# Layer 0 of a four-layer image network: where the 2x2 parity order of the pixels is made, how the row maxima are cut, and in which order a step's parts stand on each engine

## The chip, the core and the metric

The kernel runs on one core of a Trainium2 chip. The metric is the device time of one execution in microseconds (us); the time of a version is the median of three runs. One further execution is taken with the hardware profiler, and all durations below come from that one. The engines are called PE (TensorE, the matrix engine; PEld is its weight load, which overlaps the matmul before it), DVE (VectorE), ACT (ScalarE), POOL (GpSimd) and SP (SyncE, which only issues transfers).

## The reference, cut to what matters

The input `x` is 8 images of 128 channels and 56x56 pixels, float32. Four layers follow one another, each as `x = x + layer(group_norm(x))`, with 32 groups. The change touches layer 0 alone, an attention in which every window looks at four windows chosen for it:

```python
xw   = windows(gn(x))                      # 49 windows of 8x8 pixels per image, 128 channels
q, k, v = split(xw @ W_qkv + b_qkv)        # 128 channels each
logit = (q.mean(pixels) * SCALE) @ k.mean(pixels).T      # 49 x 49
r_idx = top_k(logit, 4)                    # four windows for each window
k_sel, v_sel = k[r_idx], v[r_idx]          # 4 * 64 = 256 keys
attn = softmax(q_h * SCALE @ k_sel.T)      # 8 heads of 16 channels, 64 queries x 256 keys
o    = attn @ v_sel
lepe = depthwise_3x3(image(v)) + lepe_b    # 3x3 convolution of each channel by itself
out  = (o + lepe) @ W_o + b_o
```

Layer 1 is a tanh recurrence over the 3136 pixels of an image, layer 2 a masked 3x3 convolution with a 1x1 one, layer 3 a block of two 3x3 convolutions.

## The kernel before

**Units.** `X` holds all 8 images on chip, 128 channels on the partitions. An image is 7 blocks of 448 pixels, a block one row of 7 windows; there are 56 blocks and 392 windows, worked on in 196 pairs. `xw` holds the normalised pixels of one image by windows, `kT` (called `ks` when it is read) its keys, `q` the queries of one block, once for each head of a pair of heads with the other's channels masked. The values go to memory as rows of pixels (`vpix`) and are fetched window by window into the buffer `ring`; they also go to memory as an image (`vimg`) from which the depthwise convolution is read (`v3`).

**Parity order.** Within a window the 64 pixels do not stand in reading order but sorted by the parity of row (`a`) and of column (`c`): four groups of 16. The depthwise convolution and the transposes of 32 channels need it. `normalise` (L287 to L292) makes this order as it writes `xw`, with one instruction for each of the four groups; the end of `project` (L483 to L487) takes it apart again as it adds the result to `X`, again with four.

**A step.** The loop over `p` from -3 to 201 works on several pairs at once. In step `p`:

- `scores(p+2)` (L570): PE multiplies the queries of two windows with their 256 gathered keys, for four groups of 32 channels, into four banks of PSUM called `s0` to `s3`. `maxima(p+2, g)` (L577): DVE takes the maximum over the keys, one instruction of 512 elements for each bank. `halve(p+2)` (L583, L584): POOL splits the negated maxima into two bfloat16 halves. `flip(p+2)` (L589): PE transposes them into bank `t2`; `flipped(p+2)` (L593): ACT copies them to `nm`.
- `shifted(p+1)` (L602, L612): PE writes the negated maxima of the pair before, and on top of them the transposed scores, into four banks `t0` to `t3`. `exponentials(p+1, g)` (L622): ACT, one for each bank.
- `values(p)` (L636): PE multiplies the exponentials with the fetched values, into `po`, which lies in bank `s0`. `turned` and `divide` (L648, L657, L660): DVE transposes the sums and divides by the denominators, into `ot`.
- `join(p-2)` (L465): POOL adds the depthwise result to `ot`. `back(p-2)` (L471): DVE transposes the sum into `outs`, by channels again.
- `gather(2p+6)` (L534): POOL copies the keys of the chosen windows, eight copies. `fetch(p+2)` (L549): SP, ACT and POOL issue the transfers of the chosen values.

**Jobs.** Beside these parts a step does up to one job in each of three places, `one`, `two` and `light`: the work that is done once for each block or image. A job has a part on PE and an end on other engines. Per block these are keys (L305, end on ACT L311), image (L316, end on ACT L322, then transfers), pixels (L339, end L358 on), queries (L410, end in two ACT instructions L415), depthwise (L443, end on DVE: memset L449 and transpose L451; the loads of the next block's `v3`, L429, are issued by POOL in the step after), and project (L481, end in four DVE instructions L487; the transfer `xkeep` L488 is issued by POOL in the step after). Per image come a group's mean and variance and the choice of windows. Where depthwise is placed (56 steps) it takes the place `two` and the step is called longer.

A list of jobs with the step in which each is ready and the step in which it is due is sorted by due step, and each step takes the first that is ready for each place. Instructions without a job of their own on PE (normalise, its sums L297, statistics L226 and L496) are put in steps by a weight, so that DVE's load is even.

**Order.** PE, ACT, DVE and POOL run their instructions in the order in which the program issues them (a manual schedule). Within a step that order is written out by hand in two strings, `SHORT` and, for steps with depthwise, `LONGER`. A table `SLOTS` says which bank of PSUM each part uses:

```python
SLOTS = dict(values=(ps_s, "s0"), flip=(ps_t, "t2"), one=(ps_t, "t0"), two=(ps_t, "t1"),
             light=(ps_s, "s2"), tails=(ps_s, "s1"))
SHORT = """fetch0 scores shifted gather join max0 max1 values exp0 max2 exp1 max3 halve ahead one light two flip exp2
    root back turned divide end1 exp3 flipped lit hooks tails end2 fetch1"""
```

`ahead` issues what was left over from the step before (loads of `v3`, `xkeep`), `end1` and `end2` are the ends of the jobs, `lit` that of the light one, `hooks` the instructions without a job.

Of the kernel before, what the change touches and what calls it, by code (L numbers as in the profile page):

```python
# [20 lines left out]
P = 128  # L21
# [29 lines left out]
def conv_stack_kernel(ctx: ExitStack, tc: tile.TileContext, a: dict, out: bass.AP):  # L51
# [81 lines left out]
    with ExitStack() as l0:  # L133
# [69 lines left out]
        banks = itertools.cycle([(ps, f"{k}{g}") for k, ps in (("s", ps_s), ("t", ps_t)) for g in range(4)])  # L203
# [69 lines left out]
        def preparation(b):  # L273
# [9 lines left out]
            def normalise(i, scalar=False):  # L283

                dst = xw[:, i * NW : (i + 1) * NW, :].rearrange("p j (a c u v) -> p a c u j v", a=2, c=2, u=4)
                src = X[:, b, i * BLK : (i + 1) * BLK].rearrange("p (u a j v c) -> p a c u j v", u=4, a=2, v=4, c=2)
                for k in itertools.product(range(2), range(2)):  # L287
                    to, x = dst[:, k[0], k[1]], src[:, k[0], k[1]]
                    if scalar:
                        nc.scalar.activation(to, x, AF.Identity, bias=st["off"], scale=st["r"])  # L290
                    else:
                        nc.vector.tensor_scalar(to, x, st["gm"], st["r"], ALU.subtract, ALU.mult)  # L292
# [20 lines left out]
            def image_mm(i):  # L313
                st["pv", i] = psum([P, 4 * WS // 2, NW, WS // 2], f"pvt_{b}_{i}")
                x = xw[:, i * NW : (i + 1) * NW, :].rearrange("p j (s v) -> p s j v", v=WS // 2)
                nc.tensor.matmul(st["pv", i], wvi, x, start=True, stop=True)  # L316
# [88 lines left out]
        def queries(b, i):  # L405
            st = {}

            def mm():
                st["pq"] = psum([P, BLK], f"pq_{b}_{i}")
                nc.tensor.matmul(st["pq"], wqkv[:, :P], xwf[:, i * BLK : (i + 1) * BLK], start=True, stop=True)  # L410

            def end():
                q = qs[b, i] = strip.tile([P, NW, 2, WPX], F32, name=f"q_{b}_{i}", tag="q", bufs=2)
                for h in range(2):
                    nc.scalar.activation(  # L415
                        q[:, :, h], st["pq"].rearrange("p (j x) -> p j x", x=WPX), AF.Identity,
                        bias=qbias[:, h : h + 1], scale=qscale[:, h : h + 1],
                    )
# [54 lines left out]
        def project(b, i):  # L473
# [3 lines left out]
            def mm():  # L477
                st["py"] = psum([P, 2, 2, 4, HW // 2], f"py_{b}_{i}")
                at = (b * NBLK + i) % 2 * NW
                x = outs[:, at : at + NW].rearrange("p j (s v) -> p s j v", v=WS // 2)  # L480
                nc.tensor.matmul(st["py"].rearrange("p a c u (j v) -> p (a c u) j v", v=WS // 2), wo, x, start=True, stop=True)  # L481

            def end():  # L483
                x = X[:, b, cols].rearrange("p (u a x c) -> p a c u x", u=4, a=2, c=2)
                for k in itertools.product(range(2), range(2)):
                    to, y = x[:, k[0], k[1]], st["py"][:, k[0], k[1]]
                    nc.vector.scalar_tensor_tensor(to, y, bo2, to, ALU.add, ALU.add)  # L487
# [71 lines left out]
        def scores(p):  # L559
# [3 lines left out]
                s=[ps_s.tile([P, 2, TOPK * WPX], F32, name=f"s_{p}_{g}", tag=f"s{g}") for g in range(4)],  # L563
                nmax=win.tile([P, 2, 4], F32, name=f"nmax_{p}", tag="nmax"),
            )
            for o in range(2):
                w = wins[2 * p + o]
                for g in range(4):
                    h = slice(g * CL, (g + 1) * CL)
                    nc.tensor.matmul(  # L570
                        s_["s"][g][:, o, :], w["qm"][h].rearrange("p h x -> p (h x)"), w["kw"][h],
# [3 lines left out]
        def maxima(p, g):  # L575
            s_ = pairs[p]
            nc.vector.tensor_reduce(s_["nmax"][:, :, g], s_["s"][g], AX.X, ALU.max, negate=True)  # L577
# [152 lines left out]
        for f in (image[0], image[1], *pixels[1:]):  # L730
# [3 lines left out]
                     light=(ps_s, "s2"), tails=(ps_s, "s1"))  # L734
# [9 lines left out]
        hook(-1, lambda: neighbours(0, 0))  # L744
# [10 lines left out]
        for b in range(B):  # L755
            for i in range(NBLK):
                q, last = pair_of(b, i * NW), pair_of(b, i * NW + NW - 1)
                if b or i > 1:
                    job(max(pair_of(b, i * NW - NW - 1) - 1, -1), q - 3, lambda b=b, i=i: queries(b, i))
# [1219 lines left out]
```

## Time and profile before

| | |
|---|---|
| median of three runs | 3303.14 us (3300.36 to 3306.16) |
| profiled execution | 3306.33 us |
| its span (first to last instruction) | 3304.5 us |
| mean granted clock of TensorE | 0.988 of full speed |
| layer 0 | the first 1190 us or so of the span |
| PE busy, span | 3143.1 us, 95% |
| DVE busy, span | 2327.2 us, 70% |
| POOL busy, span | 1482.2 us, 45% |
| ACT busy, span | 1280.1 us, 39% |
| in the first 1190 us: PE, DVE, POOL, ACT busy | 1081.33, 975.38, 903.43, 661.67 us |

"Busy" is the time in which an engine runs an instruction; issuing transfers, register work and waiting are not counted. Matmuls are pipelined, so that PE can be busy without being at its peak. In a row such as `L577 DVE TENSOR_REDUCE nmax<-s`, L577 is the line of the kernel, DVE the engine, and then come the operation, what it writes and what it reads. A stretch `200:1100` is given in us from the start of the span.

### The profile page before, as it was taken

Reading aid. Unit: us, or ns where it says so; the run is one execution under the profiler, and the core shown is the slowest. Engines: PE = TensorE matmul, PEld = TensorE weight load, DVE = VectorE, ACT = ScalarE, POOL = GpSimd, SP = SyncE. Lnnn points to the kernel's source line nnn. Section 1 sums busy time; section 2 is a strip of 40 time slices with the busy share of each in tenths; the row PEclk is TensorE's granted clock in tenths of the full one; section 3 lists DMA queues with packets and bytes.
Section 4 is the critical chain, followed back from the end, with each engine's and each line's share of the span. In section 5 each row is a group of like instructions: output and inputs, shape, how many; then the busy total and the mean of one; then the engine's idle time right before and its main releaser. Section 6 shows DMA issues by size and latency. Waiting matters only on the chain.

```text
span 3304.5 us, 105617 instructions
## 1 busy us (share of the span) xinstructions
PE 3143.1 (95%) x41230; PEld 2707.2 (82%) x41230; DVE 2327.2 (70%) x6160; ACT 1280.1 (39%) x2432; POOL 1482.2 (45%) x4034
## 2 busy tenths in 40 slices
PE   7999999999998889999999999999999999999998
PEld 5767767776776679999999999999999953499988
DVE  5888888888887866655555555555523257799999
ACT  4555555555565522222111111111112144455654
POOL 4788878877787743333222222222200065322221
PEclk8999999999999999999999999999999999999999
DMA  5566666656566511110000000000022156300001
GB/s 149 129 148 144 145 140 138 149 135 140 128 142 147 114 56 52 49 49 22 1 1 1 1 1 1 1 1 1 21 62 59 52 151 159 87 25 35 30 30 41
DMA packets 196045, 242.76 MB, mean 73 GB/s; under 512 B 46368, under 2 KB 140864, under 8 KB 195536
## 3 DMA queue, kind: packets, MB, share of 16 engines
q0 software_dynamic: 47104, 126.87, 15.9%
q1 hardware_dynamic: 131632, 102.06, 11.5%
q10 hardware_dynamic: 16800, 6.97, 1.0%
q8 instruction: 328, 5.37, 0.7%
q14 instruction: 181, 1.48, 0.2%
HBM read 137.21 MB, written 67.56 MB: 62 GB/s over the span
## 4 chain that ended last, share of the span: by engine, by line
PE 67%; DVE 18%; POOL 5%; issue 5%; ACT 2%; DMA 2%; ACTq 1%; POOLq 1%; DVEq 0%; SPq 0%
PE ps L1112 27%; PE q L1077 9%; PE po L1142 5%; PE po L636 5%; PE t L612 3%; PE pc L1353 3%; PE s L570 3%; PE pi L1047 3%; DVE nmax L577 2%; POOL ks L534 1%; PE pc3b L1599 1%; PE t L602 1%; PE pc L1361 1%; PE pvp L339 1%; DVE u_pc3b L1718 1%
## 5 line engine op out<-in xcount | busy, mean ns | idle before, releaser
L1112 PE MATMUL ps<-hs,w_gates 128*128 128x136 f32 x7680 | 928.8, 279 | 0.0
L1112 PEld LDWEIGHTS ps<-hs,w_gates 128*128 128x128 f32 x7680 | 911.6, 190 | 4.5
L1126 ACT ACTIVATE hs<-v 128x272 f32<-128x272 f32 x538 | 212.3, 404 | 1167.6 <-DVE v L1124 1167.4
L622 ACT ACTIVATE e<-t 128x512 f32<-128x512 f32 x784 | 431.3, 596 | 397.6 <-PE t L612 302.5
L1124 DVE TENSOR_TENSOR v<-ps,g 128x272 f32<-128x272 f32 x538 | 216.4, 411 | 495.5 <-PE ps L1112 409.2
L577 DVE TENSOR_REDUCE nmax<-s 128x2 f32<-128x512 f32 x784 | 485.4, 682 | 78.4 <-PE s L570 76.9
L1065 POOL TENSOR_TENSOR d<-inp 128x136 f32<-128x136 f32 x186 | 87.8, 472 | 789.4 <-DVE inp L1053 789.4
L534 POOL COPY ks<-kT 128x64 f32 x1568 | 293.5, 236 | 142.2 <-PE t L612 93.5
L636 PE MATMUL po<-e,ring 128*32 128x64 f32 x12544 | 250.1, 231 | 23.6 <-DVE nmax L577 13.4
L636 PEld LDWEIGHTS po<-e,ring 128*32 128x32 f32 x12544 | 220.8, 149 | 51.6 <-DVE nmax L577 19.3
L570 PE MATMUL s<-ks,q 32*128 32x256 f32 x3136 | 240.4, 409 | 10.0 <-ACT vp L362 6.1
L612 PE MATMUL t<-q,ks 32*128 32x128 f32 x6272 | 242.0, 275 | 6.4 <-issue 6.4
L612 PEld LDWEIGHTS t<-q,ks 32*128 32x128 f32 x6272 | 223.7, 190 | 11.9 <-issue 8.6
L1599 PE MATMUL pc3b<-vb,u_w2c_t 128*128 128x196 f32 x1152 | 202.2, 338 | 19.9 <-DVE vb L1580 19.9
L1599 PEld LDWEIGHTS pc3b<-vb,u_w2c_t 128*128 128x128 f32 x1152 | 198.7, 195 | 22.2 <-DVE vb L1580 22.0
L1599 PE MATMUL pc3a<-va,u_w1c_t 128*128 128x196 f32 x1152 | 199.9, 334 | 8.1 <-DVE d_pc3a L1616 4.1
L1599 PEld LDWEIGHTS pc3a<-va,u_w1c_t 128*128 128x128 f32 x1152 | 195.1, 193 | 12.0 <-issue 9.7
L1142 PE MATMUL po<-hs,xw 128*128 128x272 f32 x744 | 204.1, 397 | 0.4 <-ACT hs L1126 0.2
L570 PEld LDWEIGHTS s<-ks,q 32*128 32x128 f32 x3136 | 149.9, 188 | 45.5 <-issue 7.6
L1077 PE MATMUL q<-d,mixed 128*128 128x136 f32 x1116 | 160.2, 279 | 0.5 <-DVE g L1091 0.3
L429 POOL DMA_DIRECT2D v<-vimg x224 | 147.6, 665 | 13.7 <-issue 13.3
L1142 PEld LDWEIGHTS po<-hs,xw 128*128 128x128 f32 x744 | 132.0, 190 | 22.4 <-ACT hs L1126 1.0
(307 smaller groups left out, 5394.3 us busy)
## 6 DMA issues: line engine op xcount, KB each, us to landing
v<-vimg POOLq DMA_DIRECT2D x216, 232.0 KB
ring<-vpix SPq DMA_DIRECT2D x1176, 32.0 KB
kept<-g SPq DMA_DIRECT2D x56, 272.0 KB, 2.1
g<-kept SPq DMA_DIRECT2D x56, 272.0 KB, 2.7
xkeep<-X POOLq DMA_DIRECT2D x56, 224.0 KB
vimg<-vrow POOLq DMA_DIRECT2D x108, 116.0 KB
out_dram<-u_pc3b SPq DMA_DIRECT2D x31, 392.0 KB, 2.4
vpix<-vp POOLq DMA_DIRECT2D x42, 256.0 KB
```

What stands on the lines that cost most here:

```text
L534: nc.gpsimd.tensor_copy(kw[:, t : t + 1, :], ks[b][:, bass.ds(at, 1), :])
L570: nc.tensor.matmul(s_["s"][g][:, o, :], w["qm"][h].rearrange("p h x -> p (h x)"), w["kw"][h], start=True, stop=True,)
L577: nc.vector.tensor_reduce(s_["nmax"][:, :, g], s_["s"][g], AX.X, ALU.max, negate=True)
L612: nc.tensor.matmul(s_["t"][g][:, o, c], w["kw"][h, c * P : (c + 1) * P], w["qm"][h].rearrange("p h x -> p (h x)"), start=False, stop=(o == ...
L622: nc.scalar.activation(s_["e"][g], s_["t"][g], AF.Exp)
L636: mm = nc.tensor.matmul(po[g * CL : (g + 1) * CL, h, :, o], flat[:, at : at + 8 * CL - 7 : 8], s_["e"][g][:, o, c, h * WPX : (h + 1) * WPX ...
L1077: nc.tensor.matmul(q[n // 3][:, n % 3], w, x, start=True, stop=True)
L1112: nc.tensor.matmul(ps[f][:, i], whh[:, k, m * P : (m + 1) * P], prev[k // 2][:, (s - 1) % 2, k % 2].rearrange("p c b -> p (c b)"), start=( ...
L1124: nc.vector.tensor_tensor(v[:, i : i + n], ps[f][:, i : i + n], x, ALU.add)
L1126: nc.scalar.activation(to, x, AF.Tanh)
L1142: nc.tensor.matmul(po, wout[:, k, :], hs[k // 2][:, :, k % 2], start=(k == 0), stop=(k == KH - 1))
L1599: nc.tensor.matmul(bank[:, half].rearrange("p (y x) -> p y x", x=H4), u[:, dy, k, :], v[:, k, i * RB + dy : i * RB + dy + RB, :], start=(d ...
```

## The change

It touches layer 0 only.

- `xw`, and with it `kT`'s source, keeps the pixels of a window in reading order: `normalise` is one instruction of 448 elements instead of four of 112.
- The matmuls of image, queries and project are cut in four of 112 columns. Image and queries read `xw`, and project reads `outs`, with strides, one parity group at a time. Image writes the group to its place in the bank; project writes its bank with a step of two, so that the bank holds reading order, and its end is one instruction of 448 instead of four.
- The two ends of the queries bring `q` to parity order: the first half stays on ACT, the second half is a DVE instruction.
- The four score banks become two tiles of two banks each, `s0` and `s1`, and the maxima two instructions of 1,024 elements. `po` lies in `s0` as before, whose tile is now two banks; `light` goes from `s2` to `s1`.
- `join` and `back` work on pair `p-1` instead of `p-2`, and `join` stands ahead of `gather`.
- The strings of a step's order are written anew: `flip` ahead of the second job, `one` ahead of it in `SHORT` and `two` in `LONGER`; `turned`, `divide` ahead of `back`.
- Ready and due steps of queries, depthwise and project are moved, and `neighbours(0, 0)` by one step.

```diff
             return pe, end or (lambda: None), scalar
-        banks = itertools.cycle([(ps, f"{k}{g}") for k, ps in (("s", ps_s), ("t", ps_t)) for g in range(4)])
+        banks = itertools.cycle([(ps_s, "s0"), (ps_s, "s1")] + [(ps_t, f"t{g}") for g in range(4)])
         begun = []
         def psum(shape, name, dtype=F32):
...
             def normalise(i, scalar=False):
-                dst = xw[:, i * NW : (i + 1) * NW, :].rearrange("p j (a c u v) -> p a c u j v", a=2, c=2, u=4)
-                src = X[:, b, i * BLK : (i + 1) * BLK].rearrange("p (u a j v c) -> p a c u j v", u=4, a=2, v=4, c=2)
-                for k in itertools.product(range(2), range(2)):
-                    to, x = dst[:, k[0], k[1]], src[:, k[0], k[1]]
-                    if scalar:
-                        nc.scalar.activation(to, x, AF.Identity, bias=st["off"], scale=st["r"])
-                    else:
-                        nc.vector.tensor_scalar(to, x, st["gm"], st["r"], ALU.subtract, ALU.mult)
+                dst = xw[:, i * NW : (i + 1) * NW, :].rearrange("p j (u v) -> p j u v", v=WS)
+                src = X[:, b, i * BLK : (i + 1) * BLK].rearrange("p (u j v) -> p j u v", u=WS, v=WS)
+                if scalar:
+                    nc.scalar.activation(dst, src, AF.Identity, bias=st["off"], scale=st["r"])
+                else:
+                    nc.vector.tensor_scalar(dst, src, st["gm"], st["r"], ALU.subtract, ALU.mult)
             def sums(i):
...
             def image_mm(i):
                 st["pv", i] = psum([P, 4 * WS // 2, NW, WS // 2], f"pvt_{b}_{i}")
-                x = xw[:, i * NW : (i + 1) * NW, :].rearrange("p j (s v) -> p s j v", v=WS // 2)
-                nc.tensor.matmul(st["pv", i], wvi, x, start=True, stop=True)
+                x = xw[:, i * NW : (i + 1) * NW, :].rearrange("p j (u a v c) -> p a c u j v", u=4, a=2, c=2)
+                for k in itertools.product(range(2), range(2)):
+                    to = st["pv", i][:, 8 * k[0] + 4 * k[1] : 8 * k[0] + 4 * k[1] + 4]
+                    nc.tensor.matmul(to, wvi, x[:, k[0], k[1]], start=True, stop=True)
             def image_end(i):
...
             st = {}
             def mm():
-                st["pq"] = psum([P, BLK], f"pq_{b}_{i}")
-                nc.tensor.matmul(st["pq"], wqkv[:, :P], xwf[:, i * BLK : (i + 1) * BLK], start=True, stop=True)
+                st["pq"] = psum([P, 2, 2, 4 * NW, 4], f"pq_{b}_{i}")
+                x = xwf[:, i * BLK : (i + 1) * BLK].rearrange("p (u a v c) -> p a c u v", a=2, v=4, c=2)
+                for k in itertools.product(range(2), range(2)):
+                    nc.tensor.matmul(
+                        st["pq"][:, k[0], k[1]], wqkv[:, :P], x[:, k[0], k[1]], start=True, stop=True
+                    )
             def end():
                 q = qs[b, i] = strip.tile([P, NW, 2, WPX], F32, name=f"q_{b}_{i}", tag="q", bufs=2)
-                for h in range(2):
-                    nc.scalar.activation(
-                        q[:, :, h], st["pq"].rearrange("p (j x) -> p j x", x=WPX), AF.Identity,
-                        bias=qbias[:, h : h + 1], scale=qscale[:, h : h + 1],
-                    )
+                x = st["pq"].rearrange("p a c (j u) v -> p (a c) j (u v)", u=4)
+                to = [q[:, :, h].rearrange("p j (k x) -> p k j x", k=4) for h in range(2)]
+                nc.scalar.activation(to[0], x, AF.Identity, bias=qbias[:, 0:1], scale=qscale[:, 0:1])
+                nc.vector.tensor_scalar(to[1], x, qscale[:, 1:2], qbias[:, 1:2], ALU.mult, ALU.add)
             return fill(mm, end)
...
             st, cols = {}, slice(i * BLK, (i + 1) * BLK)
             def mm():
-                st["py"] = psum([P, 2, 2, 4, HW // 2], f"py_{b}_{i}")
+                st["py"] = psum([P, 4, 2, HW // 2, 2], f"py_{b}_{i}")
                 at = (b * NBLK + i) % 2 * NW
-                x = outs[:, at : at + NW].rearrange("p j (s v) -> p s j v", v=WS // 2)
-                nc.tensor.matmul(st["py"].rearrange("p a c u (j v) -> p (a c u) j v", v=WS // 2), wo, x, start=True, stop=True)
+                x = outs[:, at : at + NW].rearrange("p j (a c u v) -> p a c u j v", a=2, c=2, v=4)
+                for k in itertools.product(range(2), range(2)):
+                    nc.tensor.matmul(
+                        st["py"][:, :, k[0], :, k[1]].rearrange("p u (j v) -> p u j v", v=4),
+                        wo, x[:, k[0], k[1]], start=True, stop=True,
+                    )
             def end():
-                x = X[:, b, cols].rearrange("p (u a x c) -> p a c u x", u=4, a=2, c=2)
-                for k in itertools.product(range(2), range(2)):
-                    to, y = x[:, k[0], k[1]], st["py"][:, k[0], k[1]]
-                    nc.vector.scalar_tensor_tensor(to, y, bo2, to, ALU.add, ALU.add)
+                nc.vector.scalar_tensor_tensor(
+                    X[:, b, cols], st["py"].rearrange("p u a x c -> p (u a x c)"), bo2, X[:, b, cols], ALU.add, ALU.add
+                )
                 later.append(lambda: nc.gpsimd.dma_start(xkeep[b][:, cols], X[:, b, cols]))
             return fill(mm, end)
...
             s_ = pairs[p] = dict(
-                s=[ps_s.tile([P, 2, TOPK * WPX], F32, name=f"s_{p}_{g}", tag=f"s{g}") for g in range(4)],
+                s=[ps_s.tile([P, 2, 2, TOPK * WPX], F32, name=f"s_{p}_{k}", tag=f"s{k}") for k in range(2)],
                 nmax=win.tile([P, 2, 4], F32, name=f"nmax_{p}", tag="nmax"),
             )
             for o in range(2):
...
                 for g in range(4):
                     h = slice(g * CL, (g + 1) * CL)
                     nc.tensor.matmul(
-                        s_["s"][g][:, o, :], w["qm"][h].rearrange("p h x -> p (h x)"), w["kw"][h],
+                        s_["s"][g // 2][:, g % 2, o], w["qm"][h].rearrange("p h x -> p (h x)"), w["kw"][h],
                         start=True, stop=True,
                     )
-        def maxima(p, g):
+        def maxima(p, k):
             s_ = pairs[p]
-            nc.vector.tensor_reduce(s_["nmax"][:, :, g], s_["s"][g], AX.X, ALU.max, negate=True)
+            to = s_["nmax"][:, :, 2 * k : 2 * k + 2].rearrange("p o g -> p g o")
+            nc.vector.tensor_reduce(to, s_["s"][k], AX.X, ALU.max, negate=True)
         def halve(p):
...
             run(f)
         nc.scalar.activation(root, eps, AF.Exp)
         SLOTS = dict(values=(ps_s, "s0"), flip=(ps_t, "t2"), one=(ps_t, "t0"), two=(ps_t, "t1"),
-                     light=(ps_s, "s2"), tails=(ps_s, "s1"))
+                     light=(ps_s, "s1"), tails=(ps_s, "s1"))
         def second():
...
         hook(-1, lambda: tails.append(second))
         for i in range(3, NBLK):
             job(-1, min(pair_of(0, (i - 2) * NW) + 1, 2 * i), lambda i=i: image[i], True)
-        hook(-1, lambda: neighbours(0, 0))
+        hook(-2, lambda: neighbours(0, 0))
         def offset():
...
             for i in range(NBLK):
                 q, last = pair_of(b, i * NW), pair_of(b, i * NW + NW - 1)
                 if b or i > 1:
-                    job(max(pair_of(b, i * NW - NW - 1) - 1, -1), q - 3, lambda b=b, i=i: queries(b, i))
-                job(q + 1, q + 1, lambda b=b, i=i: depthwise(b, i), True, LONG)
-                job(last + 3, last + 5, lambda b=b, i=i: project(b, i), name=("project", b, i))
+                    job(max(q - 5, -1), q - 5 + (i < 4 and not b), lambda b=b, i=i: queries(b, i))
+                job(q, q, lambda b=b, i=i: depthwise(b, i), True, LONG)
+                job(last + 2, last + 4, lambda b=b, i=i: project(b, i), name=("project", b, i))
         for b in range(1, B):
             at = [FIRST + 1] * NBLK if b == 1 else [pair_of(b - 2, 0) + 2 * i - 1 for i in range(NBLK)]
...
         ih, hh = vecs[:, at : at + KH], vecs[:, at + KH : at + 2 * KH]
         hook(END // 2 + 10, lambda: nc.vector.tensor_add(bg, ih, hh))
-        SHORT = """fetch0 scores shifted gather join max0 max1 values exp0 max2 exp1 max3 halve ahead one light two flip exp2
-            root back turned divide end1 exp3 flipped lit hooks tails end2 fetch1"""
-        LONGER = """fetch0 scores shifted gather join max0 max1 values exp0 max2 exp1 max3 halve ahead two exp2 root back
-            turned divide end2 flip light one exp3 flipped lit hooks tails end1 fetch1"""
+        SHORT = """fetch0 scores shifted join gather max0 values exp0 max1 exp1 halve ahead one exp2 light flip exp3
+            flipped two root turned divide back lit end1 hooks tails end2 fetch1"""
+        LONGER = """fetch0 scores shifted join gather max0 values exp0 max1 exp1 halve ahead two exp2 light flip exp3
+            flipped one root turned divide end2 back lit hooks tails end1 fetch1"""
         def ahead(p):
             for f in later:
...
             if 0 <= p + 2 < END:
                 acts.update(scores=lambda: scores(p + 2), halve=lambda: halve(p + 2), flip=lambda: flip(p + 2),
                             flipped=lambda: flipped(p + 2))
-                for g in range(4):
-                    acts[f"max{g}"] = lambda g=g: maxima(p + 2, g)
+                for k in range(2):
+                    acts[f"max{k}"] = lambda k=k: maxima(p + 2, k)
             if 0 <= p + 1 < END:
                 acts["shifted"] = lambda: shifted(p + 1)
                 for g in range(4):
...
             if 0 <= p < END:
                 acts.update(values=lambda: values(p), root=lambda: root_table(p), turned=lambda: turned(p),
                             divide=lambda: divide(p))
-            if 0 <= p - 2 < END:
-                acts.update(join=lambda: join(p - 2), back=lambda: back(p - 2))
+            if 0 <= p - 1 < END:
+                acts.update(join=lambda: join(p - 1), back=lambda: back(p - 1))
             if p >= 0 and p + 2 < END:
                 acts.update(fetch0=lambda: fetch(p + 2, False), fetch1=lambda: fetch(p + 2, True))
             if p + 3 < END:
```

## The prediction

> **What bounds the kernel now.** I read the page first, for the whole.
>
> ```profile
> span 3304.5 us, 105617 instructions
> PE 3143.1 (95%) x41230; PEld 2707.2 (82%) x41230; DVE 2327.2 (70%) x6160; ACT 1280.1 (39%) x2432; POOL 1482.2 (45%) x4034
> ```
>
> TensorE is the bound, but only layer 0 changes, so the second view is busy time by stretch (columns: stretch, length, then busy time and instructions of PE, PEld, DVE, ACT, POOL; clock, DMA share, GB/s), and the third the instructions of the maxima.
>
> ```profile
> 200.00:1100.00 900.00, 836.34 (x20539) 636.44 (x20541) 761.68 (x1925) 515.55 (x997) 718.33 (x2287) 0.99 0.61 141
> ```
>
> ```profile
> L577 DVE TENSOR_REDUCE nmax<-s x784: 629/681/694, 37.7 to 1171.1; 128x2 f32<-128x512 f32 x196
> ```
>
> Four maxima make a step, so 196 steps take (1171.1-37.7)/195 = 5.81 us each. PE is busy 93% of them, DVE 85%, POOL 80%. To see what a step must take and what it loses, I read TensorE's timeline at a clean step:
>
> ```profile
> 629.39 1.15 PE L570 MATMUL s<-ks,q 32*128 32x256 f32 x16
> 631.68 1.27 PE L636 MATMUL po<-e,ring 128*32 128x64 f32 x64
> 632.87 1.02 PE L305 MATMUL pk<-xw,wqkv 128*128 128x448 f32 x2
> 633.73 0.92 PE L316 MATMUL pvt<-xw,wvi 128*128 128x448 f32 x2
> 634.48 0.28 PE L589 MATMUL flip<-ident,halves 128*128 128x128 bf16 x2
> 634.69 0.50 PE L570 MATMUL s<-ks,q 32*128 32x256 f32 x4
> ```
>
> By differences of starts: scores to values 2.29, values 1.19, a first job 0.86, a second 0.75, flip 0.21; together 5.30. A step with no disturbance needs 3.69 plus its jobs. Next, the timeline of all engines where queries are the second job, and what follows:
>
> ```profile
> 645.58 0.28 PE L589 MATMUL flip<-ident,halves 128*128 128x128 bf16 x2
> 645.78 1.15 PE L570 MATMUL s<-ks,q 32*128 32x256 f32 x16
> 645.94 0.37 ACT L593 COPY nm<-flip 128x256 bf16<-128x256 bf16 x1 [0.75 <-PE flip L589]
> 646.21 1.34 ACT L415 ACTIVATE q<-pq,qbias,qscale 128x448 f32<-128x448 f32 x2
> 646.86 1.07 DVE L292 TENSOR_SCALAR xw<-X,gm,r 128x112 f32<-128x112 f32 x4
> 647.61 0.39 PE L602 MATMUL t<-nm,ones 2*128 2x512 bf16 x3 [0.23 <-ACT q L415]
> 647.85 2.48 DVE L577 TENSOR_REDUCE nmax<-s 128x2 f32<-128x512 f32 x4
> 648.82 1.25 PE L636 MATMUL po<-e,ring 128*32 128x64 f32 x64
> 651.03 0.31 DVE L471 STREAM_TRANSPOSE outs<-ot 128x128 f32<-128x128 f32 x1 [0.70 <-POOL ot L465]
> 651.75 0.28 PE L589 MATMUL flip<-ident,halves 128*128 128x128 bf16 x2
> ```
>
> Scores to values now take 648.82-645.78 = 3.04: 0.75 lost, because ACT freed the queries' bank (t1) only at 647.55. Over all steps between 200 and 1,100 us, starts of scores to starts of values average 2.70, so 0.41 is lost there per step, 2.9 us per seven steps (seven steps are two blocks of 448 pixels). DVE also sits idle 0.70 for the sum (join), in all:
>
> ```profile
> DVE outs L471 <- POOL ot L465: 59.9, 73, 2.6
> ```
>
> (waits between 200 and 1,100 us: us, times, longest.)
>
> **The change, part by part.** *Split matmuls.* Images, queries and projections become four matmuls of 112 columns each, and each runs as two passes with a weight load each: eight pairs for two, 168 times (3 x 56). Columns streamed are the same. The price is the load. The row nearest to it has the same 128x128 load under few columns:
>
> ```profile
> 164.05 0.53 PEld L369 LDWEIGHTS pw<-xm,wqkv 128*128 128x128 f32 x4
> ```
>
> Four loads of 0.19 each span 0.53, so they start (0.53-0.19)/3 = 0.11 apart although only 49 columns stream behind each. Eight pairs of pixels_mm (L339, 128 columns) likewise take 0.89 as second job, 0.99 as first. I take that: +0.14 a job over 0.75 and 0.85, in all 168 x 0.14 = 23.5 us, 0.84 per seven steps. The other bound is 0 (columns alone). All of it is on PE's path. Reads now step over every second float, and the projection writes its bank so; no row shows a stepped write. The nearest rows are the depthwise patches (L443, rows of four floats) and the values' runs of 16: their steps show no extra, so I take 0, with a doubled projection (8 x 0.11 x 56 = 49 us) as the other end.
> The Trainium skill, page "PSUM — Partial Sum Buffer", section "Specifications (TRN2)", speaks against this: it says that any non-contiguous pattern in PSUM slows matmuls significantly, and lines there are 8 bytes. It gives no figure; as an estimate, one slot in two lost in the projection would be that same 49 us, where the rows give 0.
>
> *Ends.* Normalise and the projection's end become one instruction of 448 in place of four (1.07 and 1.05 us): about 0.62 each, by L297 (448 elements, 0.61). Half of queries moves from ACT (1.34 for two) to DVE, another 0.62. DVE gains 0.45+0.43 and loses 0.62 per block: 0.07 us a step. The built order shows the catch: DVE's half waits for ACT's half (same bank), ACT's half stands behind exp3 and nm, and normalise, the next maxima, and the next scores' first matmul into t0 stand behind DVE's half.
>
> *Maxima.* Two of 1,024 elements: 0.62 - 0.09 overhead = 0.53 per 512, so 2 x (1.07+0.09) = 2.32 for 2.48; DVE gains 0.16 a step. But values write the bank pair s0, so they now wait for 0.68+0.53 = 1.22 of maxima where 0.68 did: from scores' start 1.15+0.02+1.22+0.05 = 2.44 against 2.29, so +0.15 in every step that was on time, more when DVE is late. Bounds: 0 and 0.54.
>
> *Sum first, back one step on.* DVE's wait for the sum (59.9 us of 900, 0.39 a step) goes. It only buys DVE's punctuality. POOL does the same work earlier; its four v loads (2.66 us) and xkeep still stand between halve and the next gather.
>
> *Order.* Flip comes before the second job, so nm is ready 0.9 us earlier and waits for it go; the wait for halves loses that cover (3.3 us after the scores' end instead of 4.2; halves end 3.1 after it when on time). I charge 0.2 per seven steps; bounds -0.3 and 0.8.
>
> *Where lateness now goes.* In the built order queries come first in 54 steps, 22 times alone and 26 with project behind. From flip's start: nm ends at 0.73, ACT's half at 1.4, DVE's half at 2.05, normalise at 2.65. Alone: the next scores start at 0.21, values could at 2.50, but max0 ends at 2.65+1.22, so values start at 3.92: 1.42 lost. With project (0.89, end 0.62 behind normalise, to 3.27): values could at 3.39, start at 4.54: 1.15 lost. Depthwise without another job (26 steps, 46 before): memset and transpose to 0.87, back 1.18, one statistic 1.84, values at 3.11 against 2.50: 0.61 lost. Once each per seven steps that is 3.18, and 0.15 in the other four, 0.6: 3.78 against the 2.9 of before.
>
> Sum for seven steps: 0.84 + (3.78-2.9) + 0.2 = +1.9; for 28 such groups +54. The last four have no normalise: -5. At the start normalise is shorter on DVE's way to the first choice of windows (four times 0.45), and at the end the last projection comes a step earlier: together -5. Net +44 on the profiled execution, whose own time is 3306.33 (span 3304.5); the median of the runs, 3303.14, is 0.1% below it and takes the same difference: 3347.
>
> **Rivals.** *The order wins (other side).* If DVE and ACT, freed of the sum's wait, reach q early enough, both losses at q vanish: the 2.9 us shrink to 4 x 0.15+0.6 = 1.2 and work adds 0.84: -0.86+0.2 = -0.7 per seven steps, -18-10 = 3275. It decides at DVE's half of q: it must end within 0.6 us of flip for max0 to be no later than the scores. For it: DVE's 59.9 us. Against it: nm alone ends 0.73 after flip. *Loads hide behind columns,* and normalise runs at 0.4: -0.84 and -0.4 per seven steps, +0.7: 3303+20-10 = 3313. *Stepped access costs double in the projection:* 3347+49 = 3396. That the maxima are not really halved in number, or the order not kept, is excluded by the built order.
>
> **How the numbers follow.** Forecast 0.62 (its own range 3325 to 3372), hidden loads 0.10, stepped access 0.08, the order wins 0.20. The range 3275 to 3396 reaches down to the fast rival's number and up to that of the stepped ones; outside lie half of the fast rival, 0.10, and a tail above of some 0.07. A measurement here tells about 0.2%, 7 us, from no change: faster 0.20, same 0.05 (from the hidden loads' lower end), slower 0.75.
>
> **What would show it.** Right: eight matmuls of a split job spaced 0.11; PE waiting before values for maxima (L577's successor) as the largest wait, worst after queries; DVE idle before its half of q until ACT; the wait for the sum gone; steps near 6.05 us. Wrong: DVE starting max0 on time after queries; a projection longer than 1.0 us; steps at or below 5.8 us.

## The result, and the profile after

The changed kernel takes 3356.99 us (median of four runs, 3353.6 to 3359.46), against 3303.05 us of before (now of four runs, too): a ratio of 1.0162, 95% interval 1.0145 to 1.0180, so 54 us slower. The prediction was 3347 us, slower. The profiled execution took 3358.34 us with a span of 3356.5 us.

The page's first lines of the changed kernel:

```profile
span 3356.5 us, 107014 instructions
PE 3146.7 (94%) x42238; PEld 2804.0 (84%) x42238; DVE 2311.3 (69%) x5497; ACT 1251.9 (37%) x2367; POOL 1483.5 (44%) x4034
```

PE is busy 3.6 us longer, yet the span is 52 us longer: what was added is idle time. DVE has 16 us less to do, and it didn't help. The row of the maxima, and the stretch of before's second view:

```profile
L584 DVE TENSOR_REDUCE nmax<-s x392: 1161/1217/1227, 35.3 to 1226.5; 128x4 f32<-128x1024 f32 x196
200.00:1100.00 900.00, 795.40 (x20140) 674.98 (x20136) 709.34 (x1331) 469.03 (x903) 684.19 (x2164) 0.99 0.56 132
```

A step takes (1226.5 - 35.3)/195 = 6.11 us for 5.81: 0.30 more, 195 times, 58 us. All of the loss lies in layer 0: the last maximum starts 55.4 us later and the whole ends 52 us later. The first maximum comes 2.4 us earlier. PE is idle 104.6 us of 900 where it was 63.7.

PE's largest waits between 200 and 1,100 us (us, times, longest) name the place; below them DVE's, which is behind them:

```profile
PE po L643 <- DVE nmax L584: 48.8, 118, 1.4
PE t L609 <- DVE X L491: 19.5, 21, 1.5
PE t L609 <- DVE q L421: 16.3, 22, 0.8
PE flip L596 <- POOL halves L591: 14.8, 22, 1.8
DVE q L421 <- ACT q L420: 39.7, 30, 3.0
```

Before, the largest of PE's waits was for the same maxima, 11.9 us, and the one ahead of flip was small:

```profile
PE po L636 <- DVE nmax L577: 11.9, 21, 1.9
PE flip L589 <- POOL halves L584: 4.8, 9, 1.3
```

DVE's old wait for the sum (59.9 us) is gone; a wait for ACT's half of the queries, 39.7 us, is there in its place. A step with queries and projection, from the timeline of all engines (rows that don't matter here are left out):

```profile
644.48 0.29 PE L596 MATMUL flip<-ident,halves 128*128 128x128 bf16 x2
644.61 1.10 PE L485 MATMUL py<-outs,wo 128*128 128x112 f32 x8
644.86 0.37 ACT L600 COPY nm<-flip 128x256 bf16<-128x256 bf16 x1 [0.15 <-PE flip L596]
645.13 0.73 ACT L420 ACTIVATE q<-pq,qbias,qscale 128x448 f32<-128x448 f32 x1
645.63 1.15 PE L576 MATMUL s<-ks,q 32*128 32x256 f32 x16
645.89 0.74 DVE L421 TENSOR_SCALAR q<-pq,qscale,qbias 128x448 f32<-128x448 f32 x1 [0.99 <-ACT q L420]
646.55 0.73 DVE L290 TENSOR_SCALAR xw<-X,gm,r 128x448 f32<-128x448 f32 x1
646.69 0.37 PE L609 MATMUL t<-nm,ones 2*128 2x512 bf16 x1
647.20 0.67 DVE L491 SCALAR_TENSOR_TENSOR X<-py,bo,X 128x448 f32<-128x448 f32 x1
647.79 2.35 DVE L584 TENSOR_REDUCE nmax<-s 128x4 f32<-128x1024 f32 x2
647.93 0.40 PE L609 MATMUL t<-nm,ones 2*128 2x512 bf16 x3 [0.87 <-DVE X L491]
647.94 1.28 PE L619 MATMUL t<-q,ks 32*128 32x128 f32 x32
649.14 1.25 PE L643 MATMUL po<-e,ring 128*32 128x64 f32 x64
```

DVE is free and idle for 0.99 us until ACT's half ends. Then everything on DVE stands in a row behind its own half: normalise, the projection's end, the maxima. PE meets this row in two places. In the step shown it is idle 0.87 us ahead of the shifted scores (`t`), until the projection's end has read its bank; the values follow them, 0.14 us after the first maximum has ended. In most steps (124 of 147) the values wait for the first maximum itself and start within 0.1 us of its end. From the start of flip, ACT's half ends at 1.38, DVE's half starts at 1.41, the maxima at 3.31 and the values at 4.66.

### The profile page after: what moved, and what is told of

The parts are those of the page before. It is cut to its first block, busy times and chain, and to the rows that moved or that the text cites. A ratio compares the mean times of both kernels' runs of the same rounds, so it can differ in the third digit from the quotient of the medians.

```text
span 3356.5 us, 107014 instructions
## 1 busy us (share of the span) xinstructions
PE 3146.7 (94%) x42238; PEld 2804.0 (84%) x42238; DVE 2311.3 (69%) x5497; ACT 1251.9 (37%) x2367; POOL 1483.5 (44%) x4034
## 3 DMA queue, kind: packets, MB, share of 16 engines
q0 software_dynamic: 47104, 126.87, 15.5%
## 4 chain that ended last, share of the span: by engine, by line
PE 66%; DVE 23%; POOL 4%; issue 4%; ACT 1%; DMA 1%; ACTq 1%; POOLq 0%; SPq 0%; DVEq 0%
PE ps L1119 27%; PE q L1084 9%; DVE nmax L584 5%; PE po L643 5%; PE po L1149 5%; PE pc L1360 3%; PE s L576 3%; PE pi L1054 2%; PE plep L446 1%; POOL v L432 1%; PE pc3b L1606 1%; POOL ks L540 1%; PE pc L1368 1%; PE t L619 1%; PE pvt L316 1%
## 5 line engine op out<-in xcount | busy, mean ns | idle before, releaser
L584 DVE TENSOR_REDUCE nmax<-s 128x4 f32<-128x1024 f32 x392 | 460.7, 1218 | 109.7 <-PE s L576 109.5
L576 PE MATMUL s<-ks,q 32*128 32x256 f32 x3136 | 230.5, 405 | 4.7 <-ACT vp L362 4.7
L619 PE MATMUL t<-q,ks 32*128 32x128 f32 x6272 | 222.2, 274 | 0.1
L432 POOL DMA_DIRECT2D v<-vimg x224 | 146.9, 662 | 16.0 <-issue 15.5
```

The lines of the kernel that those rows point to most:

```text
L576: nc.tensor.matmul(s_["s"][g // 2][:, g % 2, o], w["qm"][h].rearrange("p h x -> p (h x)"), w["kw"][h], start=True, stop=True,)
L584: nc.vector.tensor_reduce(to, s_["s"][k], AX.X, ALU.max, negate=True)
L619: nc.tensor.matmul(s_["t"][g][:, o, c], w["kw"][h, c * P : (c + 1) * P], w["qm"][h].rearrange("p h x -> p (h x)"), start=False, stop=(o == ...
```

## The experiments

Every ratio is to the kernel before on the same chip, which had medians of 3296.9 to 3303.1 us there, so the ratios are to be compared, not the times. Beside each is its 95% interval; 0.1% is 3.3 us. Where a step is cut in two below, "scores to values" is the time from its first matmul of the scores to its first of the values, and "values to scores" that from there to the next step's first matmul of the scores, as means over 193 steps of a trace: 2.79 and 3.00 us in the kernel before, 2.92 and 3.16 in the changed one.

| version | median us | ratio |
|---|---|---|
| changed kernel | 3356.99 | 1.0162 (1.0145 to 1.0180) |
| changed, DVE's half of q first | 3318.44 | 1.0042 (1.0027 to 1.0056) |
| changed, both halves of q on ACT | 3307.14 | 1.0022 (1.0011 to 1.0032) |
| changed, DVE's half first, four maxima | 3308.33 | 1.0025 (1.0012 to 1.0037) |
| changed, both halves on ACT, flip late | 3322.35 | 1.0077 (1.0061 to 1.0093) |
| before + split matmuls, no strides | 3310.49 | 1.0021 (1.0011 to 1.0031) |
| before + two maxima | 3307.28 | 1.0012 (0.9998 to 1.0027) |
| before + sum first | 3299.62 | 0.9993 (0.9982 to 1.0004) |
| before + parity part, q on ACT | 3299.51 | 1.0000 (0.9990 to 1.0010) |
| before + order part | 3313.96 | 1.0049 (1.0031 to 1.0067) |
| before + parity + sum first | 3290.67 | 0.9981 (0.9971 to 0.9991) |
| the same + two maxima | 3295.82 | 0.9995 (0.9986 to 1.0004) |
| the same, four maxima, q split, DVE first | 3296.19 | 1.0000 (0.9991 to 1.0009) |

**The chain at the queries: two instructions swapped.**

```diff
-                nc.scalar.activation(to[0], x, AF.Identity, bias=qbias[:, 0:1], scale=qscale[:, 0:1])
                 nc.vector.tensor_scalar(to[1], x, qscale[:, 1:2], qbias[:, 1:2], ALU.mult, ALU.add)
+                nc.scalar.activation(to[0], x, AF.Identity, bias=qbias[:, 0:1], scale=qscale[:, 0:1])
```

> The changed kernel with two instructions swapped: at the end of the queries DVE's half is issued ahead of ACT's, so that ACT waits for DVE instead of DVE for ACT. Theory (the chain flip, nm, ACT's half, DVE's half, normalise, maxima is the main loss): DVE's half starts at about 0.35 us after flip instead of 1.41, so normalise and the first maximum come 1.0 us earlier in the 54 steps with queries, of which 0.7 to 1.0 reaches PE: 3357 - 38 to 54 = 3303 to 3319. Rival (order and place do not matter because PE then waits for POOL's halves or the banks instead): 3347 to 3357. Rival (the maxima's gate and the loads are the whole cost): 3350 to 3357.

1.0042 in place of 1.0162: 1.2% or 40 us went, 0.7 us for each of the 56 blocks, with the same instructions on the same engines. That is the upper end of what was expected (3303 to 3319). The timeline of all engines of that version, again at a step with queries and projection (rows left out as above):

```profile
632.30 0.28 PE L596 MATMUL flip<-ident,halves 128*128 128x128 bf16 x2
632.58 0.70 DVE L420 TENSOR_SCALAR q<-pq,qscale,qbias 128x448 f32<-128x448 f32 x1
632.68 0.37 ACT L600 COPY nm<-flip 128x256 bf16<-128x256 bf16 x1 [0.22 <-PE flip L596]
633.20 0.73 DVE L290 TENSOR_SCALAR xw<-X,gm,r 128x448 f32<-128x448 f32 x1
633.32 0.72 ACT L421 ACTIVATE q<-pq,qbias,qscale 128x448 f32<-128x448 f32 x1 [0.27 <-DVE q L420]
634.63 2.36 DVE L584 TENSOR_REDUCE nmax<-s 128x4 f32<-128x1024 f32 x2
635.91 1.10 PEld L643 LDWEIGHTS po<-e,ring 128*32 128x32 f32 x64 [0.24 <-DVE nmax L584]
635.91 1.24 PE L643 MATMUL po<-e,ring 128*32 128x64 f32 x64
```

DVE's half starts 0.28 us after flip instead of 1.41, normalise 0.90 instead of 2.07, the maxima 2.33 instead of 3.31, the values 3.61 instead of 4.66. The queue is the same, only its head no longer waits; ACT now waits 0.27. This is the chain theory, and neither rival. Over the 900 us PE's wait for the maxima falls from 48.8 to 39.4 us, and its waits for a bank at the shifted scores, behind the projection's end and the halves of the queries, from 35.8 to 15.5: more came back there than at the maxima, which the expectation had named alone.

**Both halves on ACT.**

```diff
-                nc.vector.tensor_scalar(to[1], x, qscale[:, 1:2], qbias[:, 1:2], ALU.mult, ALU.add)
+                nc.scalar.activation(to[1], x, AF.Identity, bias=qbias[:, 1:2], scale=qscale[:, 1:2])
```

> The changed kernel with both halves of the queries on ACT, as before, one behind the other. Theory (DVE's wait for ACT's half, and what stands behind it on DVE, is the loss): DVE is free 1 us earlier, so the maxima are on time, but the queries' bank is free only at 0.75 + 2 x 0.73 = 2.2 us after flip, as late as in the changed kernel: of the 1.42 and 1.15 us lost after queries some 0.2 and 0.8 go, -27 us, 3330, less than the 38 us that the swap of the halves brought. Rival (any ACT work more delays the exponentials, which set the values): 3350 to 3375.

1.0022: 1.4% or 46 us went, more than I expected. Of the 54 us, 46 come from this one moved instruction: 40 from the wait at its head, and about 6 (by the 0.20% between the two versions, whose intervals overlap a little) from its 0.74 us on DVE and ACT's wait for it. My floor, the queries' bank, was misjudged. From the traces, mean time from the scores' end to the values' start: after queries with projection and nothing else (13 or 14 steps) 2.37 in the changed kernel, 1.31 with the swap, 1.34 with both on ACT; after queries alone (14 or 15 steps) 2.96, 1.82, 1.90. After a projection the bank is not late at all, since the projection and the scores lie between flip and the matmuls that need it.

**The splitting alone.** Each of the three matmuls is written as four of 112 columns in a row, for example

```diff
-                nc.tensor.matmul(st["pq"], wqkv[:, :P], xwf[:, i * BLK : (i + 1) * BLK], start=True, stop=True)
+                for k in range(4):
+                    nc.tensor.matmul(
+                        st["pq"][:, 112 * k : 112 * k + 112], wqkv[:, :P],
+                        xwf[:, i * BLK + 112 * k : i * BLK + 112 * k + 112], start=True, stop=True,
+                    )
```

> The kernel before with one edit: the matmuls of image, queries and project are cut into four of 112 columns, without strides and with all ends as before. Theory (the load is the price): each of the 168 jobs takes 0.14 us more, by the 0.11 us pitch of eight loads, so 3303 + 23.5 = 3327, and 3320 to 3337 if the longer pitch after the values (1.03 for 0.75 in the trace of the changed kernel) counts in part. Rival (loads lie behind the columns, the extra comes from strides): 3303 to 3308, with the second job still at 0.75 us.

PE's timeline gives the price as it was put:

```profile
302.05 1.15 PE L412 MATMUL pq<-xw,wqkv 128*128 128x112 f32 x8
303.03 1.06 PE L317 MATMUL pvt<-xw,wvi 128*128 128x112 f32 x8
303.92 0.28 PE L596 MATMUL flip<-ident,halves 128*128 128x128 bf16 x2
```

0.98 as first job and 0.89 as second, where one matmul of 448 took 0.86 and 0.75: +0.13 a job. But the time rose by 0.21% only, 7 us (4 to 10), not 23.5, between what the theory and the rival had expected: over the same 900 us PE is busy 844.3 us for 836.3, and its idle time falls from 63.7 to 55.7. More than half of the added work went into time in which PE had waited.

**The parity part alone** (the functions normalise, image, queries and project of the changed kernel in the kernel before, with the second half of the queries on ACT as in the edit above).

> The kernel before with the parity part alone: one-instruction ends of normalise and project, images, queries and projections as four strided matmuls, queries ended by two strided ACT instructions; order, dues and maxima as before. Theory (loads cost, strides don't, DVE's saving is mostly slack): +7 as in the cut without strides, -0 to -10 for DVE's 0.7 us a block: 3303, between 3297 and 3312. Rival (stepped reads or writes cost on TensorE): over 3320, with project's job over 1.0 us.

1.0000: what the split costs, the rest of the part pays; as I read it that is DVE's saving (733 us busy of 900 for 762). The strides cost nothing that shows: in PE's timeline, project with strided reads and a stepped write is followed by the next job after 0.98 us, as long as a first job that is cut without strides. So it is in 42 of the 44 projections that come first between 200 and 1,100 us, with strides and without; the others waited.

```profile
314.88 1.15 PE L485 MATMUL py<-outs,wo 128*128 128x112 f32 x8
315.86 1.06 PE L412 MATMUL pq<-xw,wqkv 128*128 128x112 f32 x8
```

**The maxima alone** (tiles, maxima, their places in the strings, and light's bank, as in the change).

> The kernel before with one edit: two score tiles of two banks and two maxima of 1,024 elements, the light job in s1. Theory (values wait for a maximum twice as long): with the starts of the maxima as in the trace of before, 103 of 160 steps would start their values later, by 0.20 us a step on average, 196 x 0.20 = 40 us; DVE's 0.16 us a step gives some of it back where DVE is late (half the steps, 16 us at most): 3328, between 3315 and 3343. Rival (DVE's saved overhead is worth more than the gate): 3285 to 3303.

1.0012, with an interval that holds 1: 4 us, far less than 29 or more by the gate. PE's wait for the maxima did grow, as the theory has it, but what follows it moved up:

```profile
PE po L637 <- DVE nmax L578: 31.2, 52, 2.5
POOL halves L584 <- DVE nmax L578: 35.7, 70, 2.4
```

PE waits 31.2 us before the values instead of 11.9, while POOL waits 35.7 for the last maximum instead of 44.2. Scores to values is 0.10 us longer than before (2.89), values to scores 0.10 shorter (2.89). DVE's part of the work ends earlier and, as I read it, pays most of the gate.

**The sum first alone.**

```diff
-            if 0 <= p - 2 < END:
-                acts.update(join=lambda: join(p - 2), back=lambda: back(p - 2))
+            if 0 <= p - 1 < END:
+                acts.update(join=lambda: join(p - 1), back=lambda: back(p - 1))
```

(with `join` ahead of `gather` in both strings, and depthwise and the first neighbours one step earlier)

> The kernel before with join and back one pair later (p-1), join ahead of gather, and what that needs: depthwise and the first neighbours one step earlier. Theory (the wait for the sum only makes DVE late, and part of DVE's lateness reaches PE): DVE's 59.9 us of waits in 900 go; of the 0.41 us a step that PE loses between scores and values at most half goes: 0 to -40 us, and I take -15, 3288. Rival (gather behind join comes later and PE waits for keys, or the depthwise end collides): 3303 to 3325. Rival (all of the wait is DVE slack): 3300 to 3306.

0.9993: not to be told from nothing, where 3288 was taken. Two lines of that version's waits, between 200 and 1,100 us:

```profile
DVE outs L471 <- POOL ot L465: 15.0, 25, 1.7
PE flip L589 <- POOL halves L584: 37.7, 35, 2.7
```

DVE's wait for the sum fell from 59.9 to 15.0, and PE's for the halves rose from 4.8 to 37.7. The wait was moved: scores to values is 0.28 us shorter (2.52), values to scores 0.28 longer (3.28). This fits the rival in which all of the wait is slack on DVE.

**The order part alone** (sum first, new strings, new ready and due steps; four maxima; parity and queries as before).

> The kernel before with the order part alone: sum first, the new strings and the new ready and due steps; parity, four maxima and the queries' two ACT instructions as before. Theory (the order costs mainly together with DVE's half of the queries): 3303 to 3320, 3310 taken, with PE's waits for the halves up and those for flip's copy down. Rival (the new order is itself the loss, since the halves come too late for a flip that is first): 3330 or more.

1.0049, 16 us (10 to 22): within the expected 3303 to 3320, but more than the prediction's 0.2 us for seven steps (6 us). Against the version with the sum first alone, which this one contains, it is 0.56% or 18 us. PE's waits:

```profile
PE flip L589 <- POOL halves L584: 46.2, 48, 2.8
PE t L602 <- ACT q L415: 12.2, 19, 0.7
```

The wait for the halves is 46.2 us where it was 4.8, but 37.7 of that came with the sum first, which cost no time. What the order adds is 8.5 us of 900, 0.06 us a step, as flip loses its cover; values to scores is 0.07 longer than with the sum first alone (3.34). The wait for nm before the shifted scores (4.5 before) is no longer among PE's waits. Strings and due steps were not tried apart.

**Flip late again,** on the changed kernel with both halves on ACT:

```diff
-        SHORT = """fetch0 scores shifted join gather max0 values exp0 max1 exp1 halve ahead one exp2 light flip exp3
-            flipped two root turned divide back lit end1 hooks tails end2 fetch1"""
+        SHORT = """fetch0 scores shifted join gather max0 values exp0 max1 exp1 halve ahead one exp2 light two flip exp3
+            flipped root turned divide back lit end1 hooks tails end2 fetch1"""
```

(and the first job ahead of flip in `LONGER`)

> The changed kernel with the queries' two halves on ACT, and with flip behind the second job again (in the longer steps behind the first). Theory (what is left of the order's price is PE's wait for the halves, for which a flip that is first has no cover): PE's idle time before flip (17.8 us of 900) goes, -5 to -20 against 3307: 3297 taken. Rival (a later flip makes nm, the queries' halves on ACT and so the next bank later by the 0.9 to 1.0 us of a job, which costs as much as it brings): 3304 to 3325.

1.0077, 0.55% slower than with flip first. The rival was right: in this order the queries are in front, and a flip that is a job later makes nm and the queries' ends later by that job. PE's wait for the queries' end with flip first, and then with flip late:

```profile
PE t L609 <- ACT q L421: 13.6, 21, 0.7
PE t L609 <- ACT q L421: 28.6, 43, 0.7
```

Values to scores is 0.10 us shorter with flip late (3.05 for 3.14), as the theory had it, but scores to values 0.19 longer (2.87 for 2.68). The order's price is not cured by undoing half of it.

**Four maxima with DVE's half first.**

> The changed kernel with DVE's half of the queries first and with four maxima of 512 in four tiles again. Theory (the values' gate is now what most steps wait for, 132 of 152): on-time steps win 0.15 us, late ones lose 0.16 of DVE: -5 to -20 against the swap alone (3318), 3308 taken. Rival (as on the kernel before, the gate costs only some 4 us because the next wait is close behind): 3313 to 3320.

1.0025 against 1.0042, 6 us better, though the intervals overlap, so that it is no sure difference: by these numbers the two-bank gate costs about as much here as on the kernel before.

**Towards a better kernel.** Parity and sum first together, in the old order:

> The kernel before with the parity part (queries on ACT) and the sum first, with the old strings otherwise, the old due steps of queries and project, and four maxima. Theory (both parts only give DVE slack, and PE waits for halves and loads instead): within 0.2% of before, 3295 to 3303 where before is 3301. Rival (DVE's slack of both adds up to punctual maxima): 3285 or less.

0.9981 (0.9971 to 0.9991): 6 us faster than before, the only version whose interval lies below 1, and by less than the rival had hoped for: still the theory's "within 0.2%". With two maxima as well:

> The kernel of the run before (parity part and sum first, old order) with two maxima of 1,024 elements as well. Theory (with DVE less loaded the two maxima start on time more often, so that their gate of 0.15 us a step is what is left): 3295 to 3306, 3300 taken, no gain over four maxima. Rival (the halves come 0.16 us earlier and flip waits less, which pays for the gate): 3285 to 3293.

0.9995: no gain, and 0.14% worse than with four, with intervals that overlap. Last, the queries split over two engines with DVE first, in the version with parity and sum first; the jobs' last ends (`end2` in `SHORT`, `end1` in `LONGER`) also move ahead of `lit` and `hooks`:

> The kernel with the parity part and the sum first (old order, four maxima, 3291), with the second half of the queries on DVE, issued ahead of ACT's half, and the second job's end ahead of the hooks. Theory (the shared end is harmless where no half waits for a busy engine): the queries' bank comes free up to 0.7 us earlier in 42 steps of 170, which is at most 29 us, and DVE gets 0.74 us more per block, which takes most of it back as the half that was not late did in the changed kernel (the swap left 11 us over both halves on ACT): 3276 to 3295, 3286 taken. Rival (DVE's half, behind project's end, again stands ahead of normalise and the maxima, and this costs more than ACT's 0.7 us): 3296 to 3315.

1.0000: not the gain I took (3286), but the near edge of the rival. DVE is busy 758 us of 900 for 731, and the wait is now on ACT's side:

```profile
ACT q L421 <- DVE q L420: 38.4, 36, 2.9
```

Even where DVE's half doesn't wait for ACT's, splitting the queries gains nothing. Which of the two, DVE's added work or ACT's wait, eats the gain wasn't tried apart.

## Why the prediction was right, step by step

- **The direction and the sum.** 58 us over 195 steps is 2.07 us for seven steps, where 1.9 was predicted. Steps of 6.11 us were put near 6.05; the values' wait for the maxima as PE's largest wait, DVE idle ahead of its half of the queries, and the sum's wait gone are all in the trace. One sign of being wrong is there as well, a projection over 1.0 us: behind flip it takes 1.02 to 1.03. But image, whose write has no step, takes the same 1.03 there, so the step isn't the reason.
- **The chain at the queries** was the main step, and it is shown: from flip, ACT's half ends at 1.38 (put at 1.4), DVE's half at 2.15 (2.05), normalise at 2.80 (2.65), project's end at 3.39 (3.27), the values start at 4.66 (4.54; also the mean of 13 such steps). The small lag comes from DVE's instructions: 448 elements took it 0.73 and 0.67 us, where I took 0.62 by the sums of a window. In this step the last thing waited for was the projection's bank, 0.09 us behind the maximum, which the prediction had as the last. Where the lateness was under-sized is in the other steps. After queries alone the values start 4.31 us after flip (mean of 14) and not 3.92, after depthwise alone 3.48 (mean of 17) and not 3.11, since further DVE instructions stand ahead of the maxima in many of them, for example statistics in a step whose flip starts at 369.22 and whose values start 4.85 us later:

```profile
370.63 0.74 DVE L421 TENSOR_SCALAR q<-pq,qscale,qbias 128x448 f32<-128x448 f32 x1 [2.34 <-ACT q L420]
371.30 0.73 DVE L290 TENSOR_SCALAR xw<-X,gm,r 128x448 f32<-128x448 f32 x1
371.94 0.61 DVE L502 BATCH_NORM_STATS2 st<-X 128x6 f32<-128x448 f32 x1
372.59 0.34 DVE L504 BATCH_NORM_AGGREGATE mv<-st 128x2 f32<-128x42 f32 x1
372.85 2.29 DVE L584 TENSOR_REDUCE nmax<-s 128x4 f32<-128x1024 f32 x2
```

- **The loss of before** was read too low. Between 200 and 1,100 us scores to values is 2.78 us in the mean of all 156 steps (the median is 2.68), not 2.70, so 0.49 is lost a step and 3.4 in seven, not 2.9. With 3.4 the prediction's own sum would have come to some 3333 us. The lateness of after was put too low as well (3.78, where the trace has 4.7), so the two errors cancel in part.
- **The loads** were priced rightly (0.13 us a job for 0.14). "All of it is on PE's path" is the step that failed on the kernel before, where 7 us came of 23.5. In the changed kernel values to scores, where the jobs stand, is 0.16 us a step longer than before (3.16 for 3.00), while loads and order were put at 0.15 together; so there the loads may have come in full. A changed kernel without the splitting wasn't tried.
- **The maxima.** The built-in wait is as foreseen (in steps on time the values start 1.31 us after the scores' end, which is 2.46 after their start; 2.44 was put), and a maximum of 1,024 takes 1.22 us where one of 512 takes 0.68, as was put. But the part alone costs 4 us, not the 0.15 us a step that the sum has, 29 us for 196.
- **The order** was put at 6 us and costs 16 with the sum first in it. The bounds of -0.3 to 0.8 a group of seven (22 us) hold it.
- So the direction and the chain were understood, but that the total came within 10 us is in part luck: by the parts tried alone, loads and maxima were too dear, queries and order too cheap. The single parts add up to 0.61% (parity 0, maxima 0.12, order 0.49), and together, with the queries on ACT, they make 0.22%: the parts don't simply add.
- **The rivals.** "Stepped access costs double" is excluded by 0.98 us with and without steps. The skill's rule (the Trainium skill, page "PSUM — Partial Sum Buffer", section "Specifications (TRN2)"), that a non-contiguous pattern slows matmuls significantly, doesn't hold for a write of every second float here: float32 matmuls of 112 columns take that same 0.98 us a job. "Loads hide" is half true. "The order wins" needed DVE's half to end within 0.6 us of flip; even with the swap it ends at 0.98, and the time stays above before.

Open is which shared buffer makes one half wait for the other, the bank that both read or the tile that both write; it wasn't tried.

## What to carry to other kernels

When work is moved from a busy engine to another, look at what it waits for there: an instruction that waits at the head of a queue costs its wait to all that stand behind it. Here 0.74 us of work moved to DVE cost 0.8 us for each block, and swapping two lines gave 0.7 back. A wait taken from an engine that isn't the bound can reappear at the next one, as the sum's did ahead of flip, and the price of extra work on the bound must be set against the idle time that it has in the same step.

## What was not expected of the hardware

TensorE's reads with a step of two and writes to every second float cost nothing that a job of 0.98 us shows. Splitting a 448-column matmul in four costs 0.13 us, whatever the pattern.
